# Two cross-attention layers in fp32: the output projection of two quarters at once as a seven-product block scheme, with residual rows kept in DRAM

## The chip, the cores and the metric

The kernel runs on 1 core of one Trainium2 chip. The metric is the device time of one execution in microseconds (us). Before the change the median of three runs was 2056.8 us (2055.72 to 2058.48).

## The reference

Layer 0 is a single-head cross-attention of x (8 batches of 100 rows, width 512) to a context of 361 rows per batch. Then come two multi-head cross-attention layers (16 heads of 128) to the same context, each with a layer norm ahead and one extra bias key and value, and an MLP of width 2048. Everything is float32.

```python
x = x + alpha * (softmax(x @ wq.T @ (ctx @ wk.T).T / sqrt(512)) @ (ctx @ wv.T)) @ wo.T   # layer 0
for i in (1, 2):
    h  = layer_norm(x, ln_scale[i], ln_offset[i])
    qh = (h @ wq[i] + bq[i]).reshape(b, 100, 16, 128)
    kh = concat((ctx @ wk[i] + bk[i]).reshape(b, 361, 16, 128), bias_k[i])
    vh = concat((ctx @ wv[i] + bv[i]).reshape(b, 361, 16, 128), bias_v[i])
    w  = softmax(einsum("bqhk,bthk->bhqt", qh, kh) / sqrt(128))
    o  = einsum("bhqt,bthk->bqhk", w, vh).reshape(b, 100, 2048)
    x  = x + o @ wo[i] + bo[i]                 # the output projection: the subject of the change
h = layer_norm(x, ln_mlp_scale, ln_mlp_offset)
x = x + gelu(h @ w_fc1 + b_fc1) @ w_fc2 + b_fc2
```

## The kernel before, in words

**Stages.** Layer 0 runs first, batch by batch (`layer0_units`). The two attention layers then run in steps `(l, q, g)` (L1019): layer l, quarter q (two batches, 200 rows, `NQ`), and one of three groups g of heads. Each step has two parts j, one per batch; the text calls them k = 2g + j, 0 to 5 within a quarter. A part computes the scores of its rows (`pair_part`, L694, from products called sx, sz, sy), the softmax (`pair_exps`), transposes the probabilities on VectorE (`turned`, L331), sums column blocks of them on GpSimd (`column_sums`, L759 to L762), and mixes them with the context (`mixed`, L786, products mx, mz, my). `head_out` (L838) takes the mixed rows of a head through its value weights (product po) and writes the head into the tile oT on VectorE (L854). Scores, mixes and the MLP already use a block scheme of seven products for eight.

**The output projection.** `attn_out` (L865) runs per quarter and per block of 128 output columns: 16 heads are accumulated into one PSUM bank (pwo, L871), then ScalarE adds the bias (L872) into y. `back` (L876) turns y back to rows on TensorE, adds it to the residual rows x (L886), and `ln_stats` (L333) takes the mean and variance for the next layer norm. `normed` (L523) normalises the rows into a tile h and turns them to columns. `close_units` (L1060) is this closing of a quarter: four `attn_out` and two `back`. It stands in part k = 2 of the next quarter (L1140), and for the last quarter in the drain after the last step (L1171), ahead of the MLP.

**Order.** All the work is a list of units. A step's score units come in groups, and its other work (`fill`: projections of the next step, mixes and head products of the previous one, closings) is spread evenly between the groups (L1163 to L1169). A scheduler then orders each engine's instructions by this order as priority; `tc.high_priority(offset=-30)` puts an instruction later.

**Buffers.** Weights go through a ring "w" of six tiles of 512 KB, filled in the order of first use from the SP queue (`Ring`, L50, `load_w`, L117); wv has a ring of two. SP's queue is in order: a transfer that waits holds those behind it. PSUM is a pool of eight banks. x lives in SBUF all the time (eight tiles of 100x512, L215), oT and later half of the MLP's hidden layer g in the pool "o" with one buffer.

Of the kernel before, what the change touches and what calls it, by code (L numbers as in the profile page):

```python
# [79 lines left out]
def two_cross_attentions(ctx: ExitStack, tc: tile.TileContext, a: dict, out: bass.AP):  # L80
# [6 lines left out]
    opool = ctx.enter_context(tc.tile_pool(name="o", bufs=1))  # L87
# [10 lines left out]
    cxd = [dram.tile([P, 10 * P], F32, tag=f"cxd{b}", name=f"cxd{b}") for b in range(B)]  # L98
    wkd = {}
# [17 lines left out]
    def load_w(queue, key, t):  # L117
        kind = key[0]
        if kind in ("wq", "wqe", "wkr", "wv"):
            l, p = key[1], key[-1]  # L120
            name = {"wq": "wq", "wqe": "wq", "wkr": "wk", "wv": "wv"}[kind]
            src = rows_of(a[f"L1_xattn_{name}{l + 1}"][:, p * 2 * K : (p + 1) * 2 * K])
        elif kind == "wkT":
            if key[2] == 0:
                return
            nc.sync.dma_start(out=t, in_=wkd[key[1], key[3]])
            return
        elif kind == "wo":
            l, _, c, half = key[1:]
            src = a[f"L1_xattn_wo{l + 1}"][half * 1024 : (half + 1) * 1024, c * P : (c + 1) * P]  # L130
            src = src.rearrange("(h p) n -> p h n", p=P)
        elif kind == "f1":
            src = rows_of(a["L1_xattn_w_fc1"][:, key[2] * 256 : (key[2] + 1) * 256])
        elif kind == "f2":
            c, half = key[2:]
            src = a["L1_xattn_w_fc2"][half * 1024 : (half + 1) * 1024, c * P : (c + 1) * P]
            src = src.rearrange("(h p) n -> p h n", p=P)
        else:
            return
        return queue.dma_start(out=t.rearrange("p (c n) -> p c n", c=src.shape[1]), in_=src)  # L140
# [74 lines left out]
    xs = [const.tile([L, D], F32, tag=f"x{b}", name=f"x{b}") for b in range(B)]  # L215
# [4 lines left out]
    for b in range(B):  # L220
        (nc.sync, nc.scalar)[b % 2].dma_start(out=xs[b], in_=a["x"][b])
# [111 lines left out]
    def ln_stats(b):  # L333
        st = small.tile([L, 6], F32, tag="stats", name=f"stats_{b}")
        nc.vector.bn_stats(st, xs[b])
        nc.vector.bn_aggr(mv[:, b, :], st)
        var = small.tile([L, 1], F32, tag="var", name=f"var_{b}")
        nc.vector.tensor_scalar(var, mv[:, b, 1:2], LN_EPS, None, ALU.add)
        nc.gpsimd.tensor_tensor(rstd[:, b : b + 1], var, half, ALU.pow)
# [3 lines left out]
    xT = opool.tile([P, DT, B * L], F32, tag="o", name="xT")  # L343
    q0s = xT[:, :2, :]

    def first():
# [10 lines left out]
        for c in range(DT):  # L357
            for hf in range(2):
                pt = psum(ps_t, [P, 4 * L], f"px_{c}_{hf}")
                for n in range(4):  # L360
                    nc.tensor.transpose(
                        pt[:, n * L : (n + 1) * L], xs[4 * hf + n][:, c * P : (c + 1) * P], ident[:L, :L]
                    )
                nc.vector.tensor_copy(xT[:, c, hf * 4 * L : (hf + 1) * 4 * L], pt)
# [108 lines left out]
    def l0_out(b):  # L473
        xc = xc0.pop(b)
        ps = psum(ps_mm, [L, D], f"pd0_{b}")
        for c in range(DT):
            nc.tensor.matmul(ps, xc[:, c, :], wvo[:, c, :], start=(c == 0), stop=(c == DT - 1))
        nc.vector.scalar_tensor_tensor(xs[b], ps, alpha[:L], xs[b], ALU.mult, ALU.add)
        ln_stats(b)
# [43 lines left out]
    def normed(n, q, c):  # L523
        if c == 0:
# [8 lines left out]
            for j in range(QB):  # L533
                b = q * QB + j
                h = work.tile([L, D], F32, tag="h", name=f"h_{n}_{b}")
                nc.vector.tensor_scalar(
                    h, xs[b], mv[:, b, 0:1], rstd[:, b : b + 1], ALU.subtract, ALU.mult
                )
                hTs["rows", j] = h
# [288 lines left out]
    oTs, pbs = {}, {}  # L828
# [9 lines left out]
    def head_out(l, q, h):  # L838
        if (l, q) not in oTs:
            oTs[l, q] = opool.tile([P, H, NQ], F32, tag="o", name=f"oT_{l}_{q}")  # L840
# [5 lines left out]
        for c in range(DT):  # L846
# [8 lines left out]
            oTs[l, q][:, h, :].rearrange("p (b t) -> p b t", b=QB),  # L855
# [7 lines left out]
    ys = {}  # L863

    def attn_out(l, q, c):  # L865
        if c == 0:
            ys[l, q] = work.tile([P, DT, NQ], F32, tag="y", name=f"y_{l}_{q}", bufs=1)
        ps = psum(ps_mm, [P, NQ], f"pwo_{l}_{q}_{c}")
        for h in range(H):
            w = w8(("wo", l, q, c, h // 8))  # L870
            nc.tensor.matmul(ps, w[:, h % 8, :], oTs[l, q][:, h, :], start=(h == 0), stop=(h == H - 1))  # L871
        nc.scalar.activation(ys[l, q][:, c, :], ps, AF.Identity, bias=vec_b[:, 6 + l, c : c + 1])  # L872
# [20 lines left out]
    gs, ts, ws, mm = {}, {}, {}, {}  # L893
# [17 lines left out]
    def hidden_in(hf):  # L911
# [4 lines left out]
        g0 = opool.tile([P, 8, 2 * NQ], F32, tag="o", name=f"g_{hf}")  # L916
        g1 = zf[:, 3200:6400].rearrange("p (f t) -> p f t", f=8)
# [96 lines left out]
    def store(b):  # L1014
        nc.sync.dma_start(out=out[b], in_=xs[b])
# [9 lines left out]
    def project_units(n):  # L1025
# [8 lines left out]
        for h in range(h0, h1):  # L1034
            if q == 0 and (h % 2 == 0 or h == h0):
                key = "wkT", l, 0, h // 2
                if h % 2 == 0:
                    res.append(unit(lambda p=h // 2: wk_transposed(l, p), (W, ("wkr", l, h // 2)), (W, key)))
            res.append(unit(lambda h=h: queries(l, q, h), (W, ("wq", l, q, h // 2))))
            if later:  # L1040
                res += later
            later = [unit(lambda h=h: wide_queries(l, q, h), (W, ("wkT", l, q, h // 2)))]
            if h == ready:
                later.append(unit(lambda: pair_sums(l, q, 0, PAIRS[g][0])))
# [15 lines left out]
    def close_units(l, q):  # L1060
        res = [
            unit(lambda c=c: attn_out(l, q, c), (W, ("wo", l, q, c, 0)), (W, ("wo", l, q, c, 1)))
            for c in range(DT)
        ]
        res += [unit(lambda j=j: back(ys[l, q], j * L, q * QB + j, ln_stats)) for j in range(QB)]
        return res

    def mlp_units(hf):
        norm = [unit(lambda q=q, c=c: normed(2, q, c)) for q in (2 * hf, 2 * hf + 1) for c in range(DT)]
# [14 lines left out]
        end = [ends(2), ends(3)] + [ends(j, cs) for cs in (range(3), range(3, 4)) for j in range(2)]  # L1084
# [50 lines left out]
    for n, (l, q, g) in enumerate(steps):  # L1135
        ahead = project_units(n + 1) if n + 1 < len(steps) else []
        half_ahead = (len(ahead) + 1) // 2
        for j in range(QB):
            fill = []
            if j == 0 and n and g == 1 and (l, q) != (0, 0):  # L1140
                pl, pq, _ = steps[n - 2]
                fill += close_units(pl, pq)
# [17 lines left out]
            if l == 0 and q == 1:  # L1160
                k = 2 * g + j
                fill += e_units(1)[4 * k // 3 : 4 * (k + 1) // 3]
            groups = score_units(n, j)  # L1163
# [7 lines left out]
    drain = mix_units(n, 1) + out_units(n) + close_units(1, B // QB - 1)  # L1171
    norm, hid, mlp, end = mlp_units(0)
    norm1, hid1, mlp1, end1 = mlp_units(1)
    units += held[9:] + norm[:4] + woven(drain, norm[4:])

    def whole():
        for fn, _ in end1[:2]:
# [3 lines left out]
    units += hid + woven(mlp, norm1) + woven(hid1, end) + mlp1 + end1[2:]  # L1181
# [26 lines left out]
```

## Time and profile before

| what | value |
|---|---|
| runs | 2056.8 us median of 3 (2055.72 to 2058.48) |
| the profiled execution's own time | 2053.21 us |
| its span | 2051.4 us |
| granted TensorE clock, mean | 0.996 |
| output projection (pwo, L871) | 1024 matmul records, 175.8 us busy |
| closings in the trace | start at 424.0, 640.3, 852.6, 1070.4, 1283.2, 1493.9, 1706.2 and 1862.2 us |
| DMA | 256.94 MB, mean 125 GB/s |
| weights wo | 64 loads of 512 KB from the SP queue |

How to read it: the page gives busy time per engine (PE is TensorE's matmuls, PEld its weight loads, DVE VectorE, ACT ScalarE, POOL GpSimd, SP the queue that issues most transfers). In the groups, "x1024 | 175.8, 332 | 0.0" means 1024 instructions, 175.8 us busy, 332 ns the mean of one, 0.0 us of idle time of the engine just before them. Matmul records overlap, so 332 ns is not their pace. "<- X" names what an engine waited for. A line of a timeline gives start, length, engine, line, operation and count, and in brackets the idle time ahead of it with its releaser.

### The profile page before, as it was taken

The numbers are of one execution on the slowest core, as the hardware profiler recorded it, in microseconds if no ns is written. First come the engines' busy times: TensorE is split into PE (matmuls) and PEld (weight loads), VectorE is DVE, ScalarE is ACT, GpSimd is POOL, SyncE is SP. The second block draws the span as 40 slices with busy tenths as digits, with TensorE's granted clock in tenths as the row PEclk, the third lists the DMA queues.
The fourth block names the chain that finished last, engine by engine and source line by source line (L and its number), as shares of the span: only waits on it lengthen the run. The fifth ranks groups of instructions, "written<-read, shape, count | busy, mean of one in ns | idle before, by whom it ended". The sixth has DMA issues, their size and how long they took to land. (4 is left out here: it accounts for less than half of the span.)

```text
span 2051.4 us, 31244 instructions
## 1 busy us (share of the span) xinstructions
PE 1994.6 (97%) x11119; PEld 1822.8 (89%) x11119; DVE 1227.6 (60%) x3455; ACT 766.9 (37%) x2026; POOL 617.9 (30%) x1074
## 2 busy tenths in 40 slices
PE   9998999999999999999999999999999999989998
PEld 5668899898899989998999999989998999879998
DVE  2564776647764766466664757476647664772543
ACT  1224544424342444334433444344433442421331
POOL 3332442323242242323332332232233232323140
PEclk9999999999999999999999999999999999999999
DMA  8794235452444135424443343325332444123332
GB/s 254 250 309 149 88 88 169 128 159 73 144 148 144 54 96 158 126 70 125 148 129 120 90 155 93 120 59 180 96 123 63 146 121 133 42 64 103 114 112 65
DMA packets 254115, 256.94 MB, mean 125 GB/s; under 512 B 35756, under 2 KB 226640, under 8 KB 250632
## 3 DMA queue, kind: packets, MB, share of 16 engines
q1 hardware_dynamic: 249776, 244.58, 38.3%
q0 software_dynamic: 2112, 6.40, 0.9%
q10 hardware_dynamic: 2072, 3.97, 0.6%
q8 instruction: 88, 1.44, 0.3%
q14 instruction: 67, 0.55, 0.1%
HBM read 229.24 MB, written 25.67 MB: 124 GB/s over the span
## 5 line engine op out<-in xcount | busy, mean ns | idle before, releaser
L331 DVE STREAM_TRANSPOSE pT<-p 32x192 f32<-32x192 f32 (+1 forms) x1664 | 602.1, 362 | 84.8 <-ACT p L315 56.4
L795 PE MATMUL mx<-pT,ctx 128*128 128x256 f32 (+3 forms) x960 | 282.7, 393 | 13.3 <-DVE Z L821 5.9
L685 PE MATMUL sx<-cT,Z 128*128 128x181 f32 x1152 | 230.2, 319 | 5.5 <-DVE p L725 5.5
L795 PE MATMUL mz<-pT,ctx 105*128 105x256 f32 (+3 forms) x768 | 210.1, 396 | 10.8 <-POOL pT L759 9.4
L685 PEld LDWEIGHTS sx<-cT,Z 128*128 128x128 f32 x1152 | 196.0, 191 | 19.6 <-DVE p L725 7.8
L795 PEld LDWEIGHTS mx<-pT,ctx 128*128 128x128 f32 (+1 forms) x960 | 169.6, 190 | 36.6 <-POOL pT L761 8.6
L625 PE MATMUL pq<-hT,wq 128*128 128x200 f32 x1024 | 194.0, 333 | 2.5 <-DMA wq<-in_L_xattn_wq_dram 2.5
L641 PE MATMUL pqw<-q,wkT 128*128 128x200 f32 x1024 | 195.0, 332 | 0.0
L847 PE MATMUL po<-Z,wv 128*128 128x200 f32 x1024 | 193.9, 333 | 0.7 <-DMA wv<-in_L_xattn_wv_dram 0.7
L719 POOL TENSOR_SCALAR p<-nsb 128x1 f32<-128x1 f32 x192 | 33.3, 193 | 528.8 <-DVE pT L331 486.9
L795 PEld LDWEIGHTS mz<-pT,ctx 128*128 128x128 f32 (+1 forms) x768 | 146.0, 193 | 45.5 <-POOL pT L759 12.8
L625 PEld LDWEIGHTS pq<-hT,wq 128*128 128x128 f32 x1024 | 175.0, 189 | 8.2 <-DMA wq<-in_L_xattn_wq_dram 2.8
L641 PEld LDWEIGHTS pqw<-q,wkT 128*128 128x128 f32 x1024 | 176.2, 189 | 5.4 <-issue 0.3
L847 PEld LDWEIGHTS po<-Z,wv 128*128 128x128 f32 x1024 | 174.8, 189 | 5.4 <-issue 1.6
L739 ACT ACTIVATE p<-p,nm 128x362 f32<-128x362 f32 x192 | 114.8, 598 | 170.6 <-DVE nm L738 169.0
L871 PE MATMUL pwo<-oT,wo 128*128 128x200 f32 x1024 | 175.8, 332 | 0.0
L871 PEld LDWEIGHTS pwo<-oT,wo 128*128 128x128 f32 x1024 | 173.2, 190 | 0.0
L668 POOL TENSOR_TENSOR sums<-Z 128x256 f32<-128x256 f32 x96 | 69.9, 728 | 322.9 <-ACT Z L644 188.9
L738 DVE TENSOR_REDUCE nm<-p 128x1 f32<-128x362 f32 x192 | 101.6, 529 | 99.0 <-ACT p L730 87.4
L644 ACT COPY Z<-pqw 128x400 f32<-128x400 f32 x256 | 123.0, 489 | 73.4 <-PE pqw L641 73.2
L685 PE MATMUL sz<-cT,sums 128*128 128x181 f32 x768 | 149.3, 316 | 0.4 <-ACT p L713 0.4
L315 ACT ACTIVATE p<-p,rden 128x362 f32<-128x362 f32 (+2 forms) x216 | 129.6, 600 | 30.9 <-DVE rden L314 30.8
(353 smaller groups left out, 2897.5 us busy)
## 6 DMA issues: line engine op xcount, KB each, us to landing
wv<-in_L_xattn_wv_dram SPq DMA_DIRECT2D x64, 512.0 KB
wq<-in_L_xattn_wq_dram SPq DMA_DIRECT2D x64, 512.0 KB
wo<-in_L_xattn_wo_dram SPq DMA_DIRECT2D x64, 512.0 KB
wkT<-wkd SPq DMA_DIRECT2D x48, 512.0 KB
cT<-cTd SPq DMA_DIRECT2D x16, 1267.0 KB
f<-in_L_xattn_w_fc_dram SPq DMA_DIRECT2D x32, 512.0 KB
wkr<-in_L_xattn_wk_dram SPq DMA_DIRECT2D x16, 512.0 KB
ctx<-cxd SPq DMA_DIRECT2D x16, 512.0 KB
```

Source lines behind the costliest of these rows:

```text
L315: nc.scalar.mul(p[:rows, :n], p[:rows, :n], rden[:rows])
L331: nc.vector.transpose(dst[keys, :, :, i, :], src[i * QD : (i + 1) * QD, :, :, quarter, :])
L625: nc.tensor.matmul(ps, w[:, c, (h % 2) * K : (h % 2 + 1) * K], hTs[l, q][:, c, :], start=(c == 0), stop=(c == DT - 1),)
L641: nc.tensor.matmul(ps[:, c, :], w[:, h % 2, cc * P : (cc + 1) * P], qs[h], start=True, stop=True)
L644: nc.scalar.copy(Z[:, 2 * c2 : 2 * c2 + 2, :, h * L : (h + 1) * L], ps.rearrange("p c (b t) -> p c b t", b=QB),)
L668: nc.gpsimd.tensor_tensor(t[:, 0], a2[:, :2, :], a2[:, 2:, :], ALU.add)
L685: nc.tensor.matmul(ps[:, :KH], st["a"][a][:, c, :], st["ct"][:, blk, c, :], start=(first and c == 0), stop=(c == 1), skip_group_check=not ...
L738: nc.vector.tensor_reduce(nm, p[:, :S1], AX.X, ALU.max, negate=True)
L739: nc.scalar.activation(p[:, :S1], p[:, :S1], AF.Exp, bias=nm, accum_out=den)
L795: nc.tensor.matmul(ps, cx[:w, blk, :], pT[:w, u, :], start=first, stop=last, skip_group_check=more)
L847: nc.tensor.matmul(ps, w[:, c, (h % 2) * K : (h % 2 + 1) * K], Z[:, c, :, h * L : (h + 1) * L], start=(c == 0), stop=(c == DT - 1),)
L871: nc.tensor.matmul(ps, w[:, h % 8, :], oTs[l, q][:, h, :], start=(h == 0), stop=(h == H - 1))
```

## The change

**The projection.** Two quarters (a half, 400 rows) are projected together. O is a fixed tile `[P, i, j, 8, 200]`: i is the upper or lower eight heads, j the quarter. wo is cut for each pair of column blocks (cp and cp + 2) into A11, A12, A21, A22. Seven block products P1 to P7 of eight heads stand for eight. P1 and P2 need only the even quarter, and run during the odd one; the other five, with the sums of O that they need, run in parts k = 2 and 3 of the next even quarter. In the last half P1 and P2 run in the last step's parts k = 4 and 5, and the others in the drain. P6, P7 and P4 accumulate in one PSUM bank each.

**Weight sums.** The sums S1 to S4 of weight blocks are formed once per layer on GpSimd, in 16 pieces in all, during layer 0's (the first attention layer's) quarters 1 and 3, out of tiles of the ring "w", and are written to DRAM (wod); the products then load them from there.

**Residual rows.** x is no longer kept in SBUF. `keep_rows` (it replaces `ln_stats`) writes the rows to DRAM (xd), `load_rows` reads them for each norm and each closing. The norm is done in place. The bias-key units move from quarter 1 to quarter 2, and in quarter 0 the wide products of a head come before the next weight turn.

The MLP's g uses O in place of the pool "o" and a part of Z.

```diff
+        elif kind == "wor":
+            l, cp, ch = key[1:]
+            d = t.rearrange("p (u h n) -> p u h n", u=4, h=2)
+            for u in range(4):
+                c, row = cp + u // 2 * 2, (u % 2 * 8 + 2 * ch) * P
+                src = a[f"L1_xattn_wo{l + 1}"][row : row + 2 * P, c * P : (c + 1) * P]
+                nc.sync.dma_start(out=d[:, u], in_=src.rearrange("(h p) n -> p h n", p=P))
+            return
         elif kind == "wo":
-            l, _, c, half = key[1:]
+            l, _, cp, block = key[1:]
+            if block[0] == "S":
+                nc.sync.dma_start(out=t.rearrange("p (h n) -> p h n", h=8), in_=wod[l, cp][:, S_PLACE[block]])
+                return
+            c, half = cp + 2 * (block == "A22"), int(block[2]) - 1
...
-    xs = [const.tile([L, D], F32, tag=f"x{b}", name=f"x{b}") for b in range(B)]
+    O = const.tile([P, 2, 2, 8, NQ], F32, tag="O", name="O")
...
+    def load_rows(b, tag="h"):
+        xs[b] = work.tile([L, D], F32, tag=tag, name=f"xr_{b}_{loads[0]}")
+        loads[0] += 1
+        nc.sync.dma_start(out=xs[b], in_=xd[b])
+
+    def keep_rows(b, keep=False):
+
         st = small.tile([L, 6], F32, tag="stats", name=f"stats_{b}")
         nc.vector.bn_stats(st, xs[b])
+        nc.sync.dma_start(out=xd[b], in_=xs[b])
+        if not keep:
+            del xs[b]
...
+                h = hTs["rows", j] = xs.pop(b)
+                nc.vector.tensor_scalar(h, h, mv[:, b, 0:1], rstd[:, b : b + 1], ALU.subtract, ALU.mult)
...
-    def attn_out(l, q, c):
-        if c == 0:
-            ys[l, q] = work.tile([P, DT, NQ], F32, tag="y", name=f"y_{l}_{q}", bufs=1)
-        ps = psum(ps_mm, [P, NQ], f"pwo_{l}_{q}_{c}")
-        for h in range(H):
-            w = w8(("wo", l, q, c, h // 8))
-            nc.tensor.matmul(ps, w[:, h % 8, :], oTs[l, q][:, h, :], start=(h == 0), stop=(h == H - 1))
-        nc.scalar.activation(ys[l, q][:, c, :], ps, AF.Identity, bias=vec_b[:, 6 + l, c : c + 1])
+    OB = {(i, j): O[:, i, j] for i in range(2) for j in range(2)}
+    ys, mm = {}, {}
+
+    def weight_sums(l, cp, ch):
+        w = rings["w"].tiles["wor", l, cp, ch].rearrange("p (u n) -> p u n", u=4)
+        a11, a12, a21, a22 = (w[:, u] for u in range(4))
+        with tc.high_priority(offset=-TURN_BEHIND):
+            nc.gpsimd.tensor_tensor(a22, a21, a22, ALU.add)
+            nc.gpsimd.tensor_tensor(a21, a21, a11, ALU.subtract)
+            nc.gpsimd.tensor_tensor(a11, a22, a11, ALU.subtract)
+            nc.gpsimd.tensor_tensor(a12, a12, a11, ALU.subtract)
+        nc.sync.dma_start(
+            out=wod[l, cp][:, :, 2 * ch : 2 * ch + 2, :], in_=w.rearrange("p u (h n) -> p u h n", h=2)
+        )
+
+    def out_sums(stage):
+        if stage == 0:
+            nc.vector.tensor_tensor(OB[0, 0], OB[0, 1], OB[0, 0], ALU.subtract)
+            nc.vector.tensor_tensor(OB[1, 0], OB[1, 0], OB[1, 1], ALU.subtract)
+            nc.gpsimd.tensor_tensor(OB[0, 1], OB[0, 1], OB[1, 1], ALU.subtract)
+            nc.gpsimd.tensor_tensor(OB[1, 0], OB[1, 0], OB[0, 0], ALU.add)
+        else:
+            nc.vector.tensor_tensor(OB[1, 1], OB[1, 1], OB[0, 0], ALU.subtract)
+
+    PRODUCTS = {
+        "P1": ("A11", 0, 0), "P2": ("A12", 1, 0), "P3": ("S4", 1, 1), "P5": ("S1", 0, 0),
+        "P6": ("S2", 1, 1), "P7": ("S3", 0, 1), "P4": ("A22", 1, 0),
+    }
+
+    def attn_out(l, hf, cp, name):
...
+        more = name in ("P7", "P4")
+        if not more:
+            mm["wo", cp] = psum(ps_mm, [P, NQ], f"pwo_{l}_{hf}_{cp}_{name}")
+        ps = mm["wo", cp]
+        for h in range(8):
+            nc.tensor.matmul(
+                ps, w[:, h, :], OB[i, j][:, h, :], start=(h == 0 and not more), stop=(h == 7), skip_group_check=more
+            )
+        def plus(dst, bias, src):
+            nc.vector.scalar_tensor_tensor(dst, ps, bias, src, ALU.add, ALU.add)
+        if name == "P1":
+            nc.scalar.copy(c21, ps)
+        elif name == "P2":
+            plus(c11, up, c21)
+        elif name == "P3":
+            plus(c12, up, c21)
+        elif name == "P5":
+            nc.vector.tensor_tensor(c12, ps, c12, ALU.add)
+            plus(c22, down, c21)
+        elif name == "P6":
+            nc.vector.tensor_tensor(c12, ps, c12, ALU.add)
+        elif name == "P7":
+            nc.vector.tensor_tensor(c22, ps, c22, ALU.add)
+        else:
+            plus(c21, down, c21)
...
-    def close_units(l, q):
+    def close_units(l, hf):
+        res = [unit(lambda: out_sums(0))]
+        res += product_units(l, hf, "P3") + [unit(lambda: out_sums(1))] + product_units(l, hf, "P5", "P6", "P7")
+        fetch = [unit(lambda b=b: load_rows(b)) for b in range(hf * 4, hf * 4 + 4)]
+        last = [
+            unit(lambda j=j: back(ys[l, hf], j * L, hf * 4 + j, keep_rows)) for j in range(4)
+        ]
+        return res + fetch[:2] + product_units(l, hf, "P4") + last[:1] + fetch[2:3] + last[1:2] + fetch[3:] + last[2:]
...
-            if j == 0 and n and g == 1 and (l, q) != (0, 0):
-                pl, pq, _ = steps[n - 2]
-                fill += close_units(pl, pq)
+            k = 2 * g + j
+            if q % 2 == 0 and (l or q):
+                closing = close_units(*((l, q // 2 - 1) if q else (l - 1, 1)))
+                fill += {2: closing[:9], 3: closing[9:]}.get(k, [])
+            elif q % 2:
+                fill += {(4 if l and q == 3 else 0): product_units(l, q // 2, "P1"), (5 if l and q == 3 else 2): product_units(l, q // 2, "P2")}.get(k, [])
...
+            if l == 0 and q % 2:
+                fill = woven(fill, sums_units(q // 2)[slice(*{0: (0, 2), 1: (2, 4), 2: (4, 6), 5: (6, 8)}.get(k, (0, 0)))])
+            if g == 1 and j and n < len(steps) - 2:
+                fill.append(rows_unit((q + 1) % 4))
```

## The prediction

> **What bounds the kernel now.** I read the page's busy times first, then the groups by line, then what TensorE waited for between 205 and 1800 us (layer 0's start and the end left out), and last the instructions in order of time where the change cuts.
>
> From the page, busy time by engine, and the group that the change is about:
>
> ```profile
> PE 1994.6 (97%) x11119; PEld 1822.8 (89%) x11119; DVE 1227.6 (60%) x3455; ACT 766.9 (37%) x2026; POOL 617.9 (30%) x1074
> ...
> L871 PE MATMUL pwo<-oT,wo 128*128 128x200 f32 x1024 | 175.8, 332 | 0.0
> ```
>
> TensorE is busy 97%, and weight loads alone 89%, so it isn't only pipelined records that overlap. L871 has 1024 records for 512 products in the code (8 quarters x 4 column blocks x 16 heads): each fp32 product is two records. The group waited for nothing (0.0).
>
> What TensorE waited for in 205:1800, in us, times, longest:
>
> ```profile
> PE mz L795 <- POOL pT L759: 5.6, 6, 1.5
> PE mx L795 <- DVE Z L821: 5.6, 9, 2.0
> PE sx L685 <- ACT p L710: 5.5, 3, 3.1
> PE mx L795 <- POOL pT L761: 5.2, 7, 1.4
> PE sx L685 <- DVE p L725: 2.9, 3, 1.6
> ```
>
> With three shorter rows that is about 27 us in 1595 us: this is a kernel bound by TensorE's own work, so removed products come off the time nearly one for one, and every new wait comes on top.
>
> A closing in order of time (TensorE; start, us):
>
> ```profile
> 639.65 0.78 PE L685 MATMUL sz<-cT,sums 128*128 128x181 f32 x4
> 640.27 10.99 PE L871 MATMUL pwo<-oT,wo 128*128 128x200 f32 x64
> 651.09 0.78 PE L685 MATMUL sx<-cT,sums 128*128 128x181 f32 x4
> 651.71 0.78 PE L685 MATMUL sz<-cT,sums 128*128 128x181 f32 x4
> 652.33 10.99 PE L871 MATMUL pwo<-oT,wo 128*128 128x200 f32 x64
> 663.15 0.78 PE L685 MATMUL sx<-cT,Z 128*128 128x181 f32 x4
> ```
>
> TensorE runs two blocks of 10.8 us without a gap. In this stretch (640:666) VectorE is busy 4.27 of 26 us, ScalarE 2.90, GpSimd 8.38: the new sums have room here.
>
> And the last step of attention, where TensorE has the largest holes:
>
> ```profile
> 1814.63 1.55 PE L685 MATMUL sx<-cT,Z 128*128 128x181 f32 x4 [2.29 <-DVE p L725]
> ...
> 1836.99 0.62 PE L795 MATMUL mx<-pT,ctx 128*128 128x256 f32 x2
> 1841.46 1.58 PE L795 MATMUL mz<-pT,ctx 128*128 128x256 f32 x4 [3.85 <-POOL pT L759]
> ```
>
> The slice 1795:1846.3 has PE busy 43.53 of 51.30 us, so 7.8 us idle, at a granted clock of 0.93.
>
> **Removed products.** Per half and pair of column blocks 7 block products of 8 heads stand for 8: 4 halves x 2 pairs x 7 x 8 = 448 products for 512. Instruction order confirms 448, and no other count on TensorE changes. 64 products are 128 records. One record's pace, from the chain at the end (96 records in 16.27 us): 0.1695 us. 128 x 0.1695 = **-21.7 us**, all on the path.
>
> **Output evacuations.** Removed: 32 ScalarE activations (L872, 428 ns, 13.7 us). Added: 8 ScalarE copies and 56 VectorE operations from PSUM, of 370 ns (L1004) to 422 ns (L854): 22 us. VectorE goes from 60% to about 63%. They lie under the block products; cost zero while that cover stands. Without cover it is one operation, about 0.4 us, per product.
>
> **Sums of O** (out_sums). Three 128x1600 sums on VectorE and two on GpSimd per half. VectorE has a row of that very shape: L374, 128x1600, 1824 ns; 12 x 1.82 = 22 us. GpSimd: 728 ns for 256 columns (L668) and 1270 ns for 512 (L902) extrapolate to 3.6 us; 8 x 3.6 = 29 us. P3 doesn't need them, P5 needs the first, P6 the third. From the last head's product to P6 TensorE has P3 and P5 for both pairs (4 x 2.7 = 10.9 us) plus scores; VectorE has 15 transposes (5.4 us), two sums and two evacuations, about 10 us. So P6 comes out close to even: 0 to 2 us per half, I take 0.25, 1 us in all.
>
> Here a rule speaks against the change. The Trainium skill, page "SBUF — State Buffer", section "Who interferes with whom", says a VectorE instruction with two SBUF inputs and a GpSimd instruction that reads SBUF exclude one another for the whole instruction; all of these sums are of that kind, side by side on both engines. The trace agrees in sign: the 128x400 sum L896 takes 566 ns at least and 1293 at most, with GpSimd at work near the long ones. By the row alone VectorE's sums cost 22 us, by the rule up to 2.3 times that, 50 us, or 4.2 us each. In a closing VectorE has 21 us free, so the path keeps its 1 us, and 2 us per half go into the range. The accumulators of P6 stay open until P4, two of eight PSUM banks for about one stage more: 0 to 1 us per closing by the shortest waits above, I take 0, as the mixes hold two banks in the same way now without a row for it.
>
> **Weight sums** (weight_sums): 16 blocks x 4 GpSimd sums of 128x256 at 0.73 us, 47 us on an engine that is 30% busy, in layer 0's odd quarters. Each block also takes one of six weight buffers, 4 loads and a write-out. The write-out waits on SP for GpSimd, and behind it stand the next wq or wkT load and the probability rows for the head products. wq for heads 10 and 11 comes after such a write; its first use is dozens of TensorE groups later. Cost 0 to 2.9 us per block; I take 1 us in all, as the loads run so far ahead. Traffic: 64 loads of 512 KB become 56, and 16 loads and 16 write-outs come into two quarters (16 MB), where the DMA share is 0.2 to 0.5. The bias weights (8 loads, 64 VectorE operations of 0.34 us) go from quarter 1 to quarter 2; 22 us of VectorE over some 215 us in which it is idle 40% cost nothing, and lengthen the closing's VectorE work by 3 us a stage if they meet it (in the range of (c)). The wide products of a head now stand before the next weight turn; the wide product ahead of them (8 records, 1.4 us) covers ScalarE's 0.42 us copy, otherwise 14 heads lose 0.4 us each.
>
> **Residual rows.** 8 writes in layer 0, 16 in the closings, and 46 reads (6 and 8 for the two layers' norms, 16 in closings, 8 for each of the MLP's two uses), all on SP. In layer 0 the DMA share is 0.90 at 309 GB/s in 102:154; 1.6 MB more at that rate is 5 us at worst, I take 1. In a closing the third and fourth rows reuse the buffers of the first two: write, wait, read. VectorE's add for the third stands in order before transposes and head evacuations, so it holds them. A neighbour for the read is the wv load on the chain (512 KB):
>
> ```profile
> 1855.84 3.49 DMA wv<-in_L_xattn_wv_dram
> ```
>
> and for the write the last store: VectorE ends at 2047.4, the span at 2051.4, so under 4 us. Round trip about 7 us by the rows. The skill's "DMA: Bandwidth & Descriptors", section "Anatomy of one DMA", gives 2.0 us plus bytes over 436 GB/s, so 2.5 us each, 5 us for the round trip. VectorE has about 6 us of other work in between: held 0 us by the skill's figure, 2 to 3 us by the rows. I use the rows. TensorE has head and mix products meanwhile; I take 1 us for each of three closings, and 1 us in the drain, where the MLP's first adds queue behind four row adds (0 to 4).
>
> **Moved products.** P1 and P2 run in the odd quarter, in the last one inside the last step: 32 products, 10.8 us of TensorE work into the 51 us where 7.8 us stood idle. VectorE gets that time to catch up. Gain 0 to 7.8 us, plus about 1 us of clock; I take **-4**. Quarters' openings (0.3 to 3 us idle) may gain a little too; I take none.
>
> **Sum.** -21.7 (products) -4 (last step) +1 (sums of O) +1 (weight sums) +1 (layer 0's stores) +3 (closings) +1 (drain) = -18.7. The profiled execution took 2053.2 us (span 2051.4): 2034.5. It lies 3.6 us under the median of the runs, 2056.8, so on their scale 2056.8 - 18.7 = **2038 us**.
>
> **Rivals.**
> (a) As forecast, 2033 to 2044: 0.60.
> (b) All new waits are covered and the last step's holes close: 2056.8 - 21.7 - 6 = 2029. For: VectorE's 21 us free in a closing. Against: the row round trip has no cover on VectorE. 0.17.
> (c) The row round trips and the shared port take more: 3 us for each of three closings, 5 in the drain, 5 in layer 0, 2 per half for the sums, 4 for weight sums, with 4 won: 9 + 5 + 5 + 8 + 4 = 31, 2062 at the very worst, and with half of it 2047, where I put it. 0.14.
> (d) Slower: the weight sums' write-outs block SP. If each of 16 blocks holds the next weight load until GpSimd is done, TensorE waits its 2.9 us: 46 us, 2056.8 - 21.7 + 46 = 2081. It decides from 21.7/16 = 1.36 us per block. For: SP waits in order, and weights have six buffers. Against: in the page no weight load in attention's steady part made TensorE wait. 0.06.
> (e) No change, gain eaten exactly: 0.03. That the change wouldn't take out products is excluded by the instruction order.
>
> About 0.2% (4 us) is what a measurement of this kernel can tell from no change. Faster 0.89, same 0.04, slower 0.07. The range 2029 to 2050 leaves out (d), (e), the tail of (c) and the lower half of (b).
>
> **What would show it.** Right: pwo with 896 records and no idle time above 1 us in front; TensorE idle in the last step down to 2 to 4 us; row adds on VectorE with DMA as releaser, 2 to 3 us each closing. Wrong: wq, wkT or wv as releasers of TensorE in the odd quarters of layer 0 (rival d), head products waiting for VectorE behind a row add (c), or P6 waiting for the sum of O by several us.

## The result, and the profile after

| what | value |
|---|---|
| kernel before | 2057.6 us median of 4 (2055.7 to 2059.0) |
| changed kernel | 2039.9 us median of 4 (2038.1 to 2044.4) |
| ratio | 0.9918, 95% interval 0.9899 to 0.9936 |
| its profiled execution | 2040.29 us, span 2038.2 us |
| the changed kernel again, later, on another chip | 2043.1 us median of 6 (2037.6 to 2044.8), ratio 0.9927 (0.9911 to 0.9943) |

The change saves 14 to 18 us. 2038 was forecast, with a range of 2029 to 2050. There is one profile of the kernel before, and its execution (2053.2) lay under all four runs of before, so the two spans differ by less than the medians: 2051.4 - 2038.2 = 13.2 us. A second profile of the changed kernel (x_after) has a span of 2036.5.

From the page of the changed kernel:

```profile
PE 1974.1 (97%) x10991; PEld 1801.1 (88%) x10991; DVE 1282.4 (63%) x3523; ACT 760.0 (37%) x2002; POOL 702.0 (34%) x1146
```

TensorE has 128 records fewer (11119 - 10991) and is busy 20.5 us less. But the span fell by only 13.2: its idle time grew from 56.8 to 64.1 us. The groups of the projection, all at one line now:

```profile
L940 PE MATMUL pwo_P<-O,wo_S 128*128 128x200 f32 x512 | 89.4, 333 | 0.1
...
L940 PE MATMUL pwo_P<-O,wo_A 128*128 128x200 f32 x384 | 68.7, 333 | 0.0
```

512 and 384 make the 896 records expected, and next to nothing is waited for in front of them. The wait of a sum of O for P6 doesn't exist. What TensorE waited for, 205 to 1790 us (us, times, longest):

```profile
PE mz L827 <- POOL pT L791: 8.2, 9, 1.7
PE mx L827 <- ACT Z L836: 6.2, 4, 2.7
PE mx L827 <- DVE Z L853: 5.1, 6, 2.1
PE mx L827 <- POOL pT L793: 4.9, 6, 0.9
PE sx L717 <- DVE p L757: 3.0, 3, 2.2
```

All five have their counterpart before; the second (ScalarE's copy for a mix, L804 before) has grown from 2.1 us in 2 times. No transfer stands in the list. A closing in order of time:

```profile
674.96 2.87 PE L940 MATMUL pwo_P<-O,wo_S 128*128 128x200 f32 x16
677.67 0.78 PE L717 MATMUL sx<-cT,sums 128*128 128x181 f32 x4
678.28 0.78 PE L717 MATMUL sz<-cT,sums 128*128 128x181 f32 x4
678.90 5.58 PE L940 MATMUL pwo_P<-O,wo_A 128*128 128x200 f32 x32
684.31 0.49 PE L972 MATMUL pb<-ident,y 128*100 128x128 f32 x3
```

P7 and P4, with scores between them, run without a gap. So where is the idle time? The stages below begin with the first score of each quarter (before: 173.6, 351.4, 571.0, 783.4 us and so on; changed: 174.4, 356.9, 555.5, 786.7) and with the first product of the last closing (1862.2 and 1837.7). Length of the stage less TensorE's busy time, in us:

| stage | before | changed | changed, second profile | four rows ahead | rows of quarter 3 | bias units in quarter 1 | both row edits |
|---|---|---|---|---|---|---|---|
| up to quarter 0 | 12.1 | 11.5 | 14.0 | 12.0 | 12.0 | 11.7 | 11.3 |
| layer 0, quarter 0 | 5.0 | 8.4 | 6.4 | 7.6 | 7.1 | 8.4 | 7.7 |
| layer 0, quarter 1 | 10.0 | 1.9 | 1.9 | 1.9 | 1.9 | 17.7 | 1.9 |
| layer 0, quarter 2 | 2.1 | 13.1 | 13.1 | 12.0 | 8.3 | 2.9 | 8.0 |
| quarter 3, layer 1's quarters 0 to 2 | 10.6 | 10.1 | 10.0 | 7.5 | 9.3 | 11.1 | 8.0 |
| layer 1, quarter 3, up to its closing | 9.9 | 9.3 | 9.6 | 9.9 | 9.4 | 9.3 | 9.8 |
| last closing (the drain) and MLP | 7.1 | 9.9 | 10.0 | 7.6 | 9.2 | 9.9 | 7.3 |
| sum | 56.8 | 64.1 | 65.0 | 58.4 | 57.1 | 71.0 | 54.0 |

(Rounded; the last four columns are experiments, below.) The expectations below speak of a window 640:850 as quarter 2, where idle time went from 2.1 to 8.9 us. That window begins with part k = 2 of quarter 2 and runs into quarter 3, so it misses TensorE's holes at 572 and 577 us. By whole quarters quarter 2 grew by 11.0 us and quarter 1 shrank by 8.1. Layer 0 up to the end of quarter 0 grew by 2.8, the last stage by 2.8.

**The drain.** VectorE, then the SP queue, then TensorE, changed kernel:

```profile
1866.53 1.29 DVE L976 TENSOR_TENSOR xr<-pb,xr 100x512 f32<-100x512 f32 x2 [0.41 <-PE pb L972]
...
1873.80 0.69 DVE L976 TENSOR_TENSOR xr<-pb,xr 100x512 f32<-100x512 f32 x1 [2.65 <-DMA xr<-xd]
1874.40 0.57 DVE L1044 TENSOR_TENSOR O<-pgy,O 128x400 f32<-128x400 f32 x1
```

```profile
1867.25 0.91 SPq L368 DMA_DIRECT2D xd<-xr  x2
1870.90 1.09 SPq L362 DMA_DIRECT2D xr<-xd  x3
```

```profile
1877.75 1.18 PE L1031 MATMUL pgy<-hT,f 128*128 128x200 f32 x6
1882.31 2.86 PE L1031 MATMUL pgx<-ht,f 128*128 128x200 f32 x8 [3.38 <-DVE O L1052]
1884.96 2.01 PE L1031 MATMUL pgz<-ht,fs 128*128 128x200 f32 x8
1886.80 1.52 PE L1031 MATMUL pgx<-ht,fs 128*128 128x200 f32 x8
```

The third row add begins 6.6 us after the first one ends (about 1867.2): write at 1867.25, read at 1870.90, landed at 1873.80. Behind it on VectorE queue the MLP's first adds, and TensorE stands 3.38 us. Then its clock is low: eight records take 2.86 and 2.01 us where 1.52 is normal, another 1.8 us. (In the second profile the hole is 3.22 us, and the clock after it stays at 1.00.)

**Quarters 1 and 2.** The bias-key units stood in quarter 1 and stand in quarter 2 now, and the idle time went with them. Both quarters before, then changed (the columns are stage, length, then busy us of TensorE, weight loads, VectorE, ScalarE, GpSimd; granted clock; DMA share; GB/s):

```profile
351.40:571.00 219.60, 209.62 (x1169) 194.07 (x1169) 145.07 (x475) 84.22 (x226) 69.97 (x124) 1.00 0.42 131
571.00:783.40 212.40, 210.30 (x1170) 195.63 (x1169) 132.86 (x371) 85.20 (x226) 64.23 (x118) 0.99 0.37 114
```

```profile
356.90:555.50 198.60, 196.73 (x1098) 182.62 (x1097) 130.27 (x371) 85.81 (x224) 88.78 (x150) 1.00 0.50 153
555.50:786.70 231.20, 218.08 (x1209) 201.46 (x1208) 156.51 (x501) 82.64 (x222) 81.34 (x128) 0.99 0.47 141
```

The kernel before already paid for these units in quarter 1. TensorE's waits don't name them, but VectorE's do (before, 351.4:571.0; us, times, longest):

```profile
DVE wqe L563 <- DMA wqe<-in_L_xattn_wq_dram: 17.5, 4, 8.5
```

VectorE at the start of quarter 2, and at 766, changed kernel:

```profile
564.96 0.35 DVE L752 TENSOR_TENSOR p<-sz,p 128x180 f32<-128x180 f32 x1 [0.41 <-PE sz L717]
571.18 0.29 DVE L595 SCALAR_TENSOR_TENSOR wqe<-wqe,dk 128x128 f32<-128x128 f32 x1 [5.87 <-DMA wqe<-in_L_xattn_wq_dram]
...
766.14 0.67 DVE L571 TENSOR_SCALAR xr<-xr,mv,rstd 100x512 f32<-100x512 f32 x1 [3.98 <-DMA xr<-xd]
```

The bias-key units stand in VectorE's order ahead of score work. The first one waits 5.9 us for its weights, and TensorE 2.2 and 2.1 us for a score and a mix behind it (572 and 577). Their buffers "h" are the ones that residual rows use now: the rows at 766 (for layer 1's first norm) were only asked for at 760.2, half a microsecond after the last bias sum at 759.7, and came six later.

### The profile page after: what moved, and what is told of

Read it like the earlier page. It is cut to its first block, busy times and chain, and to the rows that moved or that the text cites. A ratio compares the mean times of both kernels' runs of the same rounds, so it can differ in the third digit from the quotient of the medians.

```text
span 2038.2 us, 31454 instructions
## 1 busy us (share of the span) xinstructions
PE 1974.1 (97%) x10991; PEld 1801.1 (88%) x10991; DVE 1282.4 (63%) x3523; ACT 760.0 (37%) x2002; POOL 702.0 (34%) x1146
## 4 chain that ended last, share of the span: by engine, by line
PE 73%; DVE 13%; DMA 5%; ACT 4%; POOL 3%; issue 2%; SPq 0%; DVEq 0%; POOLq 0%; ACTq 0%
PE sx L717 9%; PE mx L827 8%; PE mz L827 7%; PE pwo_P L940 7%; PE pq L657 7%; DVE pT L354 6%; PE po L877 6%; PE pqw L673 6%; PE sz L717 4%; PE my L827 3%; PE sy L717 2%; PE pfx L1080 2%; DMA xr<-xd 2%; PE sc L470 2%; PE pgx L1031 2%
## 5 line engine op out<-in xcount | busy, mean ns | idle before, releaser
L751 POOL TENSOR_SCALAR p<-nsb 128x1 f32<-128x1 f32 x192 | 37.4, 214 | 532.7 <-DVE pT L354 490.2
L717 PEld LDWEIGHTS sz<-cT,sums 128*128 128x128 f32 x768 | 124.7, 189 | 1.7 <-ACT p L745 1.6
L827 PE MATMUL my<-pT,ctx 128*128 128x256 f32 (+3 forms) x384 | 102.9, 389 | 0.0
```

Of the source, the lines that this page charges most:

```text
L717: nc.tensor.matmul(ps[:, :KH], st["a"][a][:, c, :], st["ct"][:, blk, c, :], start=(first and c == 0), stop=(c == 1), skip_group_check=not ...
L827: nc.tensor.matmul(ps, cx[:w, blk, :], pT[:w, u, :], start=first, stop=last, skip_group_check=more)
```

## The experiments

Each is the changed kernel with the edit shown. Groups of four ran on one chip each; groups are compared by their ratios to the kernel before, and 0.0010 is 2.1 us. The changed kernel's own two ratios are 0.9918 and 0.9927.

**1. Bias-key units back in quarter 1 (x_bias_q1).**

```diff
-            if l == 0 and q == 2:
+            if l == 0 and q == 1:
                 fill += e_units(1)[4 * k // 3 : 4 * (k + 1) // 3]
```

> The changed kernel with one edit: the bias-key units go back from quarter 2 of layer 0 to quarter 1. Theory A (the move of these units is what made TensorE wait in quarter 2: idle 8.9 us of 640:850 in the changed kernel, 2.1 before, because 22 us of VectorE work and the row loads meet the closing): quarter 2 falls to about 3 us idle, quarter 1 rises from 6.5 to 8 or so, time 3 to 6 us less, about 2035. Rival B (the four row adds with their statistics and the row round trip hold VectorE there, whatever else stands in the quarter): quarter 2 stays at 6 us or more, quarter 1 gets 2 to 4 us more, time equal or up to 4 us more.

Measured 2053.1 us, ratio 0.9977 (0.9970 to 0.9984): 10 to 12 us longer. Quarter 2 fell from 13.1 to 2.9 us idle, as A said, but quarter 1 rose from 1.9 to 17.7. Its granted clock is 0.95 besides. VectorE and TensorE there:

```profile
391.90 0.29 DVE L595 SCALAR_TENSOR_TENSOR wqe<-wqe,dk 128x128 f32<-128x128 f32 x1 [4.25 <-DMA wor<-in_L_xattn_wo_dram]
```

```profile
394.33 0.88 PE L717 MATMUL sx<-cT,Z 128*128 128x181 f32 x4 [3.77 <-DVE p L757]
396.45 2.07 PE L827 MATMUL mx<-pT,ctx 128*128 128x256 f32 x4 [1.24 <-DVE Z L853]
398.32 2.87 PE L673 MATMUL pqw<-q,wkT 128*128 128x200 f32 x8
```

This wait of a bias unit ends with a load for the weight sums (releaser wor), which shares SP's queue with its own. Of the 17.7 us, 10.7 are holes behind VectorE and 5.1 behind GpSimd, which forms the weight sums. So both theories fall in the time: the units cost quarter 2 about 10 us, and about 16 in quarter 1 as it is now, where the kernel before paid some 8. That the weight sums make the difference between 8 and 16 is argued from these rows; no run has the units in quarter 1 without them.

**2. All four rows ahead of P4 (x_rows_four).**

```diff
-        xs[b] = work.tile([L, D], F32, tag=tag, name=f"xr_{b}_{loads[0]}")
+        if tag == "O":
+            xs[b] = O[:L, 1, 1].rearrange("p h t -> p (h t)")[:, b % 2 * D : (b % 2 + 1) * D]
+        else:
+            xs[b] = work.tile([L, D], F32, tag=tag, name=f"xr_{b}_{loads[0]}")
...
-        fetch = [unit(lambda b=b: load_rows(b)) for b in range(hf * 4, hf * 4 + 4)]
+        fetch = [unit(lambda b=b: load_rows(b, "h" if b % 4 < 2 else "O")) for b in range(hf * 4, hf * 4 + 4)]
...
-        return res + fetch[:2] + product_units(l, hf, "P4") + last[:1] + fetch[2:3] + last[1:2] + fetch[3:] + last[2:]
+        return res + fetch + product_units(l, hf, "P4") + last
```

> The changed kernel with one edit: in every closing all four residual rows are loaded ahead of P4, the third and fourth into a part of O that is free by then, so that no row waits for another's write. Theory A (the drain's 3.4 us wait of TensorE for VectorE comes from the third row's write, wait and read): row adds wait for no DMA (5.2 us in 4 times now), the 3.4 us wait is under 1 us, time 3 to 4 us less, about 2036. Rival B (VectorE is late there by its own four adds and statistics, 6.6 us): the wait stays at 2 us or more, time within 1 us.

Measured 2031.9 us, ratio 0.9877 (0.9863 to 0.9892): 8 to 10 us less. VectorE in the drain:

```profile
1863.35 1.29 DVE L979 TENSOR_TENSOR xr<-pb,xr 100x512 f32<-100x512 f32 x2 [0.41 <-PE pb L975]
...
1865.83 0.66 DVE L979 TENSOR_TENSOR O<-pb,O 100x512 f32<-100x512 f32 x1
...
1867.18 0.68 DVE L979 TENSOR_TENSOR O<-pb,O 100x512 f32<-100x512 f32 x1
```

All four adds are over in 4.5 us where they took 9.8 (1866.53 to 1876.3), and TensorE's longest wait for L1055 (the same add) is 0.7 us. Theory A, and by more than it said: of 5.7 us less idle time 2.3 lie in the last stage, and 1.1, 0.4 and 1.8 in the quarters with the three closings. Another 1.4 us is busy time, in the drain by the clock: in 1860:1910 it is 1.00 here and 0.97 in the changed kernel. The spans differ by 7.1 us, and by 5.4 from the changed kernel's second profile, so part of the 8 to 10 is scatter.

**3. All sums of O on VectorE (x_sums_dve).**

```diff
-            nc.gpsimd.tensor_tensor(OB[0, 1], OB[0, 1], OB[1, 1], ALU.subtract)
-            nc.gpsimd.tensor_tensor(OB[1, 0], OB[1, 0], OB[0, 0], ALU.add)
+            nc.vector.tensor_tensor(OB[0, 1], OB[0, 1], OB[1, 1], ALU.subtract)
+            nc.vector.tensor_tensor(OB[1, 0], OB[1, 0], OB[0, 0], ALU.add)
```

> The changed kernel with one edit: all five sums of O of a half on VectorE, none on GpSimd. Theory A (VectorE and GpSimd shut each other out over their SBUF inputs: 1.82 us alone, up to 5.2 us side by side): every 128x1600 sum on VectorE takes 1.82 us, together 20 x 1.82 = 36 us in place of about 33 us for 12 now, GpSimd loses 32 us, TensorE's waits stay, time within 2 us. Rival B (the sums are on the path, as P5 or P6 waits for them): VectorE's two more sums come in front of P5, pwo_P gets idle time ahead of it of 1 us or more per half, time 4 us or more longer.

Measured 2041.8 us, ratio 0.9932 (0.9917 to 0.9947), which is not told apart from the changed kernel. Two of the sums in the changed kernel, then here (minimum/median/maximum of four, in ns):

```profile
L916 DVE TENSOR_TENSOR O<-O x4: 1825/3362/4904, 632.5 to 1838.4; 128x1600 f32<-128x1600 f32 x4
L920 DVE TENSOR_TENSOR O<-O x4: 1815/2236/5175, 636.7 to 1843.7; 128x1600 f32<-128x1600 f32 x4
```

```profile
L916 DVE TENSOR_TENSOR O<-O x4: 1824/1825/1826, 634.5 to 1843.3; 128x1600 f32<-128x1600 f32 x4
```

With GpSimd out of it the same sum takes 1.82 us every time. VectorE does eight sums more and is busy 1282.8 us for 1282.4; GpSimd saves 26 us. A, and the path doesn't notice.

**4. P1 and P2 of the last half at parts 0 and 2 (x_p12_even).**

```diff
-                fill += {(4 if l and q == 3 else 0): product_units(l, q // 2, "P1"), (5 if l and q == 3 else 2): product_units(l, q // 2, "P2")}.get(k, [])
+                fill += {0: product_units(l, q // 2, "P1"), 2: product_units(l, q // 2, "P2")}.get(k, [])
```

> The changed kernel with one edit: P1 and P2 of the last half at parts 0 and 2 of the last quarter, as in the other halves, and not at 4 and 5. Theory A (as forecast: they fill holes of the last step): idle time of the last step grows by 3 to 4 us, time 3 to 4 us longer, 2043. Rival B (they stand ahead of the holes, at 1748 to 1788, and the holes, 5 us at 1790 to 1838, stay what they are): last step's idle within 1 us, time within 1 us.

Measured 2045.5 us, ratio 0.9947 (0.9935 to 0.9959): 4 to 6 us longer (spans: 2.1). TensorE's longest holes in the last step, this kernel and then the changed one:

```profile
1794.30 0.88 PE L717 MATMUL sx<-cT,Z 128*128 128x181 f32 x4 [2.28 <-DVE p L757]
...
1820.98 1.13 PE L827 MATMUL mz<-pT,ctx 128*128 128x256 f32 x4 [2.34 <-POOL pT L791]
```

```profile
1805.92 0.70 PE L827 MATMUL mx<-pT,ctx 128*128 128x256 f32 x2 [1.35 <-ACT Z L844]
...
1817.28 1.73 PE L827 MATMUL mz<-pT,ctx 128*128 128x256 f32 x4 [2.34 <-POOL pT L791]
```

The products late in the quarter take away the score's wait for VectorE (2.28), not the one for the last mix. But the changed kernel has two holes of 1.7 us at 1730 and 1769 that this one lacks. Layer 1's quarter 3 up to its closing takes 213.0 us here and 209.7 there, 11.3 and 9.3 us of it idle. So theory A holds in the time; its reason, holes that are filled, gives only 2.0 of these 3.3 us.

**5. Quarter 3's norm rows in a part of O (x_rows_q3).** `load_rows` as in 2, and

```diff
-                fill.append(rows_unit((q + 1) % 4))
+                fill.append(rows_unit((q + 1) % 4, "O" if l == 0 and q == 2 else "h"))
```

> The changed kernel with one edit: the rows for quarter 3's norm in layer 0 are loaded into a free part of O and not into the two buffers that the bias-key units use too. Theory A (at 762 us VectorE waits 4.0 us for these rows, whose load was issued only at 760.2 when the bias-key units had let go of the buffer; ScalarE's copies queue behind it and TensorE stands 1.3 and 1.6 us): the wait of VectorE is gone, TensorE's holes at 762 to 768 too, time 2 to 4 us less. Rival B (quarter 2's idle time comes from the bias sums themselves in VectorE's order): within 1.5 us.

Measured 2035.0 us, ratio 0.9900 (0.9887 to 0.9913): 4 to 6 us less, though the intervals overlap at their edges. But the expectation named the wrong rows. Those that VectorE waits for at 762 belong to layer 1's first norm and keep their buffer; they still wait (4.6 us), and TensorE still has a hole of 1.2 us behind them. The edit brings quarter 3's rows from 706 to 651, and so frees the buffer for the bias units, whose last sum moves from 759.7 to 755.5. Quarter 2's idle time falls from 13.1 to 8.3 us.

**6. Bias sums with a lower priority (x_bias_late80).**

```diff
-        bias_sums(l, p, dk[:, 0, :], False)
+        with tc.high_priority(offset=-80):
+            bias_sums(l, p, dk[:, 0, :], False)
```

> The changed kernel with one edit: the bias-key units' sums on VectorE get a lower priority (80 places later), their place in the list stays quarter 2. Theory A (they stand in VectorE's order ahead of score work and hold it, 5.9 us at 565 for the load of wqe, and 2.2 us of their own at 703.5 ahead of the exponent's maximum; TensorE then stands 2.2 and 2.1 us at 572 to 577 and 2.7 us at 705): these holes go, 4 to 7 us less. Rival B (the buffers that they hold longer make the row loads of quarter 3's norm still later): no gain or up to 4 us longer, with VectorE's wait for rows above 4 us in quarter 2.

Measured 2043.6 us, ratio 0.9938 (0.9926 to 0.9950): 2 to 4 us longer, which is not told apart from the changed kernel. The wait for wqe moves and grows (from 9.6 to 12.0 us in quarter 2), TensorE's holes stay (2.2 us at 576, 2.7 at 712), and quarter 2 has 14.0 us idle. Theory A is out. No gain is what rival B said, but its reason isn't seen: the rows wait 4.3 us here and 4.4 in the changed kernel.

**7. No weight sums (x_no_wsums).**

```diff
-            if l == 0 and q % 2:
+            if False:
                 fill = woven(fill, sums_units(q // 2)[...])
...
-            if block[0] == "S":
-                nc.sync.dma_start(out=t.rearrange("p (h n) -> p h n", h=8), in_=wod[l, cp][:, S_PLACE[block]])
-                return
-            c, half = cp + 2 * (block == "A22"), int(block[2]) - 1
+            c, half = cp + 2 * (block == "A22"), int(block[-1]) % 2
```

> The changed kernel without the weight sums: the 16 pieces are not loaded, formed or written, and the S products take raw blocks of wo (the output is not that of the reference; TensorE's work is the same). Forecast's step (1 us in all for weight sums, at most 2.9 us per block): time 0 to 2 us less. Rival (the extra loads and write-outs crowd the ring and SP in layer 0's odd quarters, so that loads for others come late): 4 us or more less, with the holes of TensorE at 572 to 577 and the idle time of quarters 1 and 3 smaller.

Measured 2043.4 us, ratio 0.9936 (0.9924 to 0.9948). GpSimd is busy 654.5 us for 702.0, the 47.5 us of the sums, and nothing comes of it: no gain. Quarters 1 and 3, where the rival looked for less, have 3.0 and 3.1 us idle for 1.9 and 2.4. The stall for wqe at the start of quarter 2 remains (4.4 us in two waits).

**8. P3 twice (x_p3_twice).**

```diff
-        for h in range(8):
+        twice = 2 if name == "P3" else 1
+        for n in range(8 * twice):
+            h = n % 8
             nc.tensor.matmul(
-                ps, w[:, h, :], OB[i, j][:, h, :], start=(h == 0 and not more), stop=(h == 7), skip_group_check=more
+                ps, w[:, h, :], OB[i, j][:, h, :], start=(n == 0 and not more), stop=(n == 8 * twice - 1), skip_group_check=more
```

> The changed kernel with P3's eight products done twice into the same bank (its value doubled, so the output is not that of the reference): 4 halves x 2 pairs x 8 = 64 products, 128 records more on TensorE, nothing else, which is the number that the change removed. Theory A (a product on this path is worth its full pace, 0.1695 us a record): +21.7 us, 2061 to 2062. Rival B (in a closing TensorE has slack, since VectorE's row adds and sums hold what comes after): P3's second pass gives VectorE time and costs less, +12 to +17 us.

Measured 2063.1 us, ratio 1.0035 (1.0022 to 1.0047): 22 to 24 us longer; spans 2060.5 - 2038.2 = 22.3 us for 128 records. Theory A.

**9. The changed kernel again (x_after).**

> The changed kernel itself, once more, beside the others of this group: its first result rests on four runs (2038.1 to 2044.4), which is too few to hold differences of 2 us against. Theory A (the forecast's size was right): 2038 to 2042 us, ratio to the kernel before 0.991 to 0.993. Rival B (the first four were low, and the runs without the weight sums and with the sums on VectorE, 2042 to 2043 us, are its true level): 2042 to 2045 us, ratio 0.993 to 0.995.

Measured 2043.1 us, ratio 0.9927. The time is B's, the ratio A's, so it doesn't decide; the ten runs of the two sets have a median of 2041.4.

**10. Both row edits (x_combo).** Edit 2, and quarter 3's norm rows in `O[:L, 0, 1]`.

> The changed kernel with two edits at once: all four rows of a closing loaded ahead of P4 (third and fourth into a free part of O), and quarter 3's norm rows of layer 0 in another free part of O. Theory A (the two take away different holes: the drain's 3.4 us and chance waits behind rows in closings, and 3 us in quarter 2): the gains add, 2039.9 - 8 - 4 = 2028 us, a ratio of about 0.986, the drain's wait under 1 us and quarter 2's idle time about 6 us. Rival B (both only shift where TensorE waits for VectorE): as the better of the two alone, 2032.

Measured 2026.2 us, ratio 0.9848 (0.9833 to 0.9863): 14 to 16 us less than the changed kernel, which is the sum of the two within the noise. Its quarter 2 and its last stage (quarter 2 of the changed kernel stands above, its last stage below):

```profile
555.90:779.00 223.10, 215.07 (x1209) 200.52 (x1208) 155.82 (x501) 83.53 (x222) 80.97 (x128) 1.00 0.48 147
1826.60:2023.20 196.60, 189.29 (x1127) 184.79 (x1126) 94.28 (x146) 43.33 (x105) 54.55 (x38) 1.00 0.42 124
```

```profile
1837.70:2038.20 200.50, 190.62 (x1127) 186.54 (x1126) 96.50 (x146) 43.77 (x105) 54.49 (x38) 0.99 0.40 121
```

TensorE's longest wait for the adds in the drain is 0.6 us. Quarter 2 has 8.0 us idle, and 3.9 in the window 640:850 that the expectation means.

**11. The same for every odd quarter (x_combo_even).**

```diff
-                fill.append(rows_unit((q + 1) % 4))
+                fill.append(rows_unit((q + 1) % 4, "h" if q % 2 else "O0"))
```

> As the combination of the two edits, with the norm rows of every odd quarter in the free part of O, in both layers. Theory A (a row load that waits for no other user of its buffer is always covered): 1 to 2 us less than the combination. Rival B (only the quarter with the bias-key units has a crowded buffer): within 1 us of it.

Measured 2025.0 us, ratio 0.9844 (0.9828 to 0.9860). Not told apart from 10; the lowest time of the study.

**12. P2 of the last half in the drain (x_combo_p2).**

```diff
-                fill += {(4 if l and q == 3 else 0): product_units(l, q // 2, "P1"), (5 if l and q == 3 else 2): product_units(l, q // 2, "P2")}.get(k, [])
+                fill += {(5 if l and q == 3 else 0): product_units(l, q // 2, "P1"), (9 if l and q == 3 else 2): product_units(l, q // 2, "P2")}.get(k, [])
...
-    drain = mix_units(n, 1) + out_units(n) + close_units(1, 1)
+    drain = mix_units(n, 1)[:1] + product_units(1, 1, "P2") + mix_units(n, 1)[1:] + out_units(n) + close_units(1, 1)
```

> The combination of the two edits, with P1 of the last half at part 5 and P2 in the drain, between the last mixes. Theory A (what products gain there is the filling of holes: 1.35, 2.3 and 0.8 us of TensorE stand empty between 1805 and 1835 in the changed kernel): 2 to 4 us less than the combination. Rival B (these holes are bound by the chain from scores over VectorE's transposes and GpSimd's sums to the last mixes, which P2 in front of it only delays): within 1 us or longer.

Measured 2026.5 us, ratio 0.9852 (0.9831 to 0.9874): rival B. The 2.3 us wait for the last mix stays; P2 does not fill it.

## Why the prediction was right, step by step

**Removed products, -21.7: right.** 128 records put back cost 22.3 us (8). A record is worth its pace here; the closing has no slack that would swallow it.

**Last step, -4: about right in size, wrong in mechanism.** By (4) the late place of P1 and P2 is worth 3.3 us of the quarter, and 4 to 6 us by the ratios. But the holes were not filled: idle time of the last quarter up to its closing went from 9.9 to 9.3 us only. In the last 51.3 us ahead of the closing it fell from 7.6 to 5.4 us, not to the 2 to 4 that the forecast asked for, and two new holes of 1.7 us stand earlier. The products run at 1748 to 1788, ahead of most of the holes.

**Sums of O, +1: nothing, though single sums were slower than both bounds.** I put 1.82 us by the row and 4.2 us by the Trainium skill's rule ("SBUF — State Buffer", "Who interferes with whom"). Where both engines had a sum at hand VectorE's took 4.90 and 5.17 us; all twelve took 32.6 us, between the 22 and the 50. The rule itself held; my use of it was at fault: I scaled by a factor from a smaller sum (1293 over 566 ns), while one engine waits for the other's whole instruction. Its end is the sum of both, 1.82 + 3.57 = 5.4 us, and the runs lie under that. That cost no time on the path: P6 waited for nothing, and (3) changed nothing.

**Weight sums, +1, and rival (d): nothing.** No weight load made TensorE wait in the odd quarters, and without the sums (7) no time is gained. But they were not free in another way: with the bias units beside them in quarter 1 the kernel takes 10 to 12 us more (1).

**Layer 0's row stores, +1, and the new order in quarter 0, put at nothing: more, and in part open.** Up to the end of quarter 0 TensorE was idle 17.1 us before; in the 13 profiles of the changed kernel and its experiments it is 18.0 to 21.7. Part of it is a read that the forecast didn't price: the rows for the next norm. VectorE waits 3.5 us for them at 181, and TensorE has a hole of 1.2 us behind it at 183; where that wait is 1.8 us or less, the hole is missing. No run takes the stores or the new order away, so the rest stays open.

**Closings +3 and drain +1: the mechanism was right, the drain's term too small.** The round trip is 6.6 us, as the rows said (7), not the 5 worked out from the Trainium skill's "DMA: Bandwidth & Descriptors", "Anatomy of one DMA". That section gives its fit for transfers that GpSimd issues; these go through SP's queue, so it was an estimate beyond what the page states. VectorE waited 1.2, 0.3 and 1.1 us in the three closings, where I had 2 to 3, and 2.65 in the drain. Taking the round trips away (2) gives back 3.3 us of idle time in the closings' quarters, for the 3 that I took, and 2.3 in the last stage, for the 1. In the profiled execution the drain's hole is 3.4 us, with 1.8 of low clock behind it.

**What failed: the bias-key units, whose move was put at nothing.** I set 22 us of VectorE work against VectorE's mean idle share, and left a clash to rival (c). But an idle share does not hide these units: they stand in VectorE's order with waits of their own (5.9 us for wqe), and what TensorE needs stands behind them. The kernel before paid for that too (17.5 us of such waits in quarter 1), which I did not look up, as I read TensorE's waits alone. So the move took 8.1 us of idle time out of quarter 1 and put 11.0 into quarter 2: a net of 2.9 us. The two buffers that the units share with the residual rows now are enough to explain the surplus: with quarter 3's rows elsewhere (5) quarter 2 comes down from 13.1 to 8.3. How much of the remaining hole at 705 us (2.1 us in 10) is their VectorE work, and how much the four row adds just ahead of it, stays open: (6) didn't separate them.

So idle time was forecast to change by -4 + 7 = +3 us and changed by +7.3 (+8.2 in the second profile); busy time was to change by -21.7 and changed by -20.5 (-23.1). All of this is against the one profile of the kernel before, a fast execution; by the medians the gain is larger. The certain term, the removed products, carried the forecast. That it came so close was luck in part: two changes of 8 and 11 us that it did not have nearly cancelled, and weight sums and sums of O, which cost nothing, made up for the drain. The likeliest case (a) is what came, with row trips of rival (c) in the drain.

## What to carry to other kernels

When a tile is moved from on-chip memory to DRAM, list who else uses the buffers that the reads will take: the price here was not the bytes but a read that could be asked for only when an unrelated unit let go of its buffer. Look for a larger tile that is dead at that time (here half of O); this and an earlier fetch were worth nearly as much again as the change itself (ratio 0.9918 to 0.9848). A unit with a load of its own is not hidden by an engine's idle share: count what stands behind it in that engine's order while it waits. When such a unit is moved, its cost moves too, so price both places. And read the waits of the engines behind the bottleneck as well as its own. Compare stages between events of the program, not between fixed times.

## What the runs showed of the hardware

A hole of 2 to 4 us on TensorE often costs more than itself, but not every time. After the 2.69 us hole at 705 us in the changed kernel the granted clock of the next 4 us was 0.57:

```profile
704.00:708.00 4.00, 1.39 (x7) 0.89 (x5) 3.46 (x21) 1.51 (x5) 0.07 (x1) 1.00 0.07 14
708.00:712.00 4.00, 3.92 (x12) 3.39 (x13) 0.42 (x1) 0.70 (x4) 0.00 (x0) 0.57 0.87 303
712.00:716.00 4.00, 4.00 (x23) 3.82 (x22) 2.82 (x8) 2.35 (x6) 0.00 (x0) 1.00 0.00 0
```

12 records fit in where the next 4 us hold 23, so about 2 us are lost again. Without the weight sums (7) a hole of the same 2.69 us stands ahead of the same product, and the clock behind it stays at 1.00, with 21 records:

```profile
706.71:710.71 4.00, 4.00 (x21) 3.78 (x22) 0.95 (x2) 2.01 (x7) 0.00 (x0) 1.00 0.84 298
```

So there is no sharp limit. In the 14 traces, between 150 and 2000 us, TensorE has 37 holes of 2.3 to 3.9 us, and after 27 of them the clock of 2 of the next 4 us fell under 0.9; of 31 holes of 1.9 to 2.3 us it did after 12. What decides it the runs don't show. At some 2 us each, such falls can be part of the scatter between executions; that is argued, not shown. The Trainium skill's "TensorE: Matmul & The Clock Gate", "Part 1: The HAM clock gate", has the clock fall after at least one idle window of some 3.4 us; here less was enough, and the measurement decides.
